# Splitting the output projection of the last three query blocks by head pair in a GroupNorm + attention kernel

## The chip, the cores and the metric

The kernel runs on one core of a Trainium2 chip. The time is device microseconds of one execution; the figure given is the median of the timed runs. A separate profiled execution gives the trace, whose span is a few microseconds shorter than the timed median.

The engines are named as in the profile: PE is TensorE, DVE VectorE, ACT ScalarE, POOL GpSimd, SP SyncE (it issues most transfers). PEld is the loading of weights on TensorE.

## The reference

The input x has the shape (4, 512, 48, 48): four images, 512 channels, T = 2304 positions. Eight heads of 64 channels each.

```python
hn  = group_norm(x, groups=32) * gn_scale + gn_bias
qkv = (einsum('oc,bchw->bohw', qkv_w, hn) + qkv_b)      # fp32
q, k, v = split(qkv.reshape(b, 3, 8, 64, T).astype(float16))
s   = 64 ** -0.25
w   = softmax(einsum('bhct,bhcs->bhts', q * s, k * s))  # T x T per head
a   = einsum('bhts,bhcs->bhct', w, v).astype(float32).reshape(x.shape)
out = einsum('oc,bchw->bohw', proj_w, a) + proj_b
return x + out
```

The change concerns the last two lines: the output projection, its bias and the residual.

## The kernel before

**Tiling.** Two heads form a pair that fills the 128 partitions. There are 4 pairs in each of 4 batches, numbered g = 0 to 15. The queries of a pair are cut into five blocks: j = 0 to 3 with 512 columns and j = 4 with 256. The keys are cut into 18 tiles of 128 rows. A *unit* is three score tiles of one block: matmuls of keys and queries into `ps` (L892), three exponentials of 128x1024 on ACT into `p` (L899), a sum over the key tiles kept on DVE in `acc` (L950, L953), and the matmuls of values into `av` (L917). A block has six units (the last block three), a pair 27, the program 432. A name such as 14_2_5 means pair 14, block 2, unit 5; a slot is the stretch of PE from that unit's scores to the scores of the next.

**The loop.** The list `stream` holds all units in order. Step n issues the scores of unit n, the `acc` addition of unit n-1 and the values of unit n-2 (`BEHIND` = 2). The space beside it is filled by `fill(n)`: it takes *pieces* from the list `beside` in the order in which they were put there, at most one chain that ends per call, at a rate that spreads the remaining work over the units left until it is needed. Every piece has a unit before which it may not start. The pieces are halves of the chains for q and k of a later pair (`qk_chain`, L696), for v (`v_chain`, L741), copies of attention outputs, and projection chains. Between pieces `fill` also runs due transfers and small tasks.

**After the last unit of a block.** `add_up` (L970) sums `acc` over the partitions with matmuls against ones into `sl`; DVE copies it to `slx` (L980); small transfers bring the sums to the layout `sums` (L984); POOL checks their limits (L1008, L1009); DVE inverts them (L1015); a transfer writes `row` to DRAM (L1017), and a second one reads it back, spread over 64 partitions per head, as `ib` (L1027). POOL then multiplies `avx` (the copy of `av`) by `ib` into `att` (L1034). These steps are spread over four later loop steps.

**Projection.** For one block of a batch, `att32` (L813) casts the fp16 `att` of the four pairs to fp32r tiles `a`. Before the change one work tile `a32` with room for all four pairs and with one buffer serves every block except blocks 3 and 4 of the last batch (`at_end`), whose copies lie in freed x tiles. A projection chain is eight matmuls for 128 output channels: four pairs, each with a high and a low half of the weight, `whi` and `wlo` (L819). It goes into one PSUM bank: the single bank of `ps_w` during attention, or a bank of the score tiles when the flag `alone` is set. The evacuation on DVE (L839) adds bias and residual in one pass; the store goes out on SP one step later (L846). The residual is loaded on SP into a tile `r` by `residual`, one chain ahead of its use (L791). The 256-column block packs two output chunks into one bank, so it has two chains of sixteen matmuls.

**The order in the last batch.** The projection of the third batch's blocks runs beside pairs 14 and 15. It is followed by the last batch's own blocks 0, 1 and 2, each released a few steps after the last pair's block is divided. Blocks 3 and 4 come partly or wholly after the last unit: `alone[0] = True`, the last values, `add_up` of the last block, and then the rest of `beside`. In the last pair, blocks 3 and 4 are divided without the way through DRAM (`direct`, L991 to L993): DVE takes the reciprocal of the sums at full width, and POOL or DVE multiplies.

**The end.** The results of the sums check in `fine` are reduced on DVE (L1326), summed over partitions by a matmul (L1328), and compared into `flag` (L1329). A branch on that flag chooses whether the general, slower softmax has to be run; it isn't taken with these inputs.

Of the kernel before, what the change touches and what calls it, by code (L numbers as in the profile page):

```python
# [26 lines left out]
P = 128  # L27
# [440 lines left out]
def fast_path(  # L468
# [113 lines left out]
    fine = const.tile([P, 2, QB // P], F32, name="fine")  # L582
# [197 lines left out]
    def residual(b, j, chunks):  # L780
        n = QBLOCKS[j][1]
        if at_end(b, j):

            tag = f"x{chunks[0]}_{j - NQ + 2}"
            xt = xpool.tile([P, QB], F32, tag=tag, name=f"r_{b}_{j}_{chunks[0]}")
        else:
            xt = work.tile(
                [P, QB], F32, tag="res", bufs=3, name=f"r_{b}_{j}_{chunks[0]}"
            )
        xt = xt.rearrange("p (m n) -> p m n", n=n)  # L790
        nc.sync.dma_start(xt, rows_of(x, b, j, chunks))  # L791
        res[b, j, chunks[0]] = xt

    def at_end(b, j):

        return b == B - 1 and j >= NQ - 2

    def att32(b, j, pairs=range(NC)):
        o, n = QBLOCKS[j]
        if (b, j) not in at32:  # L800
            if at_end(b, j):
                at32[b, j] = [
                    xpool.tile([P, n], F32R, tag=f"x{c}_{j}", name=f"a32_{b}_{j}_{c}")
                    for c in range(NC)
                ]
            else:
                t = work.tile(
                    [P, NC, QB], F32R, tag="a32", bufs=1, name=f"a32_{b}_{j}"
                )
                at32[b, j] = [t[:, c, :n] for c in range(NC)]  # L810
        for c in pairs:
            engine = nc.vector if direct(b * NPAIR + c, j) else nc.gpsimd
            engine.tensor_copy(at32[b, j][c], atts[b * NPAIR + c][:, o : o + n])  # L813

    def proj_chain(b, j, m, ps):
        n = QBLOCKS[j][1]
        for c in range(NC):
            for i, w in enumerate((whi, wlo)):
                nc.tensor.matmul(  # L819
                    ps[:, :n],  # L820
                    w[:, c, bass.ts(m, P)],
                    at32[b, j][c],
                    start=(c == 0 and i == 0),
                    stop=(c == NC - 1 and i == 1),
                )

    def proj_pieces(b, j):


        n = QBLOCKS[j][1]  # L830

        def run(chunks):
            bank = chain_bank(f"pr_{b}_{j}_{chunks[0]}")
            places = [bank[:, i * n : (i + 1) * n] for i in range(len(chunks))]
            for m, ps in zip(chunks, places):
                proj_chain(b, j, m, ps)
            xt = res.pop((b, j, chunks[0]))
            for i, m in enumerate(chunks):
                nc.vector.scalar_tensor_tensor(  # L839
                    xt[:, i], places[i], bproj[:, m : m + 1], xt[:, i], ALU.add, ALU.add  # L840
                )

            loads.append(
                (
                    now[0] + 1,
                    lambda: nc.sync.dma_start(rows_of(out, b, j, chunks), xt),  # L846
                )
            )

        def ahead(k):  # L850
            if k < len(proj_list) and not at_end(b, proj_list[k][0]):
                residual(b, *proj_list[k])

        convert = [
            piece(0.0, lambda: att32(b, j, (NC - 1,) if at_end(b, j) else range(NC)))
        ]
        chains = []
        for k, (jj, chunks) in enumerate(proj_list):
            if jj != j:
                continue  # L860
            chains.append(
                [piece(0.0, lambda k=k: ahead(k)) for k in ([0] if k == 0 else [])]
                + [piece(0.0, lambda k=k: ahead(k + 1))]
                + [piece(QB / 290.0, lambda chunks=chunks: run(chunks), True, True)]
            )
        return convert, chains
# [35 lines left out]
    def values(u):  # L902
        g, j, k, last = u
        b, pr = divmod(g, NPAIR)
        o, n = QBLOCKS[j]
        per = QB // n
        pt = pts.pop(u)
        if k == 0:
            if j == 0:
                atts[g] = apool.tile([P, T], F16, tag="att", name=f"att_{g}")  # L910
            av[0] = ps_av.tile([P, QB], F32, tag="av", name=f"av_{g}_{j}")
        for r in range(BURST):
            for a in range(per):
                i = (k * BURST + r) * per + a
                for h in range(2):
                    lo = h * D
                    nc.tensor.matmul(  # L917
                        av[0][lo : lo + D, :n],
                        vv[b, pr // 2][:, i, pr % 2 * P + lo : pr % 2 * P + lo + D],
                        pt[:, r, h, a * n : (a + 1) * n],  # L920
                        start=(i == 0),
                        stop=(i == NT - 1),
                    )
        if last:
            avx[g, j] = work.tile([P, QB], F32, tag="avx", name=f"avx_{g}_{j}")
            nc.vector.tensor_copy(avx[g, j][:, :n], av[0][:, :n])  # L926

    def direct(g, j):

        return g == NG - 1 and j >= NQ - 2  # L930

    def add(u):
# [6 lines left out]
        if direct(g, j) and (last or j == NQ - 1):  # L939
            acc[g, j].append(pt)  # L940
            return
# [14 lines left out]
    def add_up(g, j):  # L956
# [3 lines left out]
        sl = ps_av.tile([P, QB], F32, tag="av", name=f"sl_{g}_{j}")  # L960
# [6 lines left out]
        for i, (t, r, a) in enumerate(steps):  # L967
            for h in range(2):
# [7 lines left out]
                )  # L976

        def rows():
            sx = work.tile([P, QB], F32, tag="rows", name=f"slx_{g}_{j}")
            nc.vector.tensor_copy(sx[:, :n], sl[:, :n])  # L980

            sm = small.tile([P, 2, QB // P], F32, tag="sums", name=f"sums_{g}_{j}")
            for h in range(2):
                nc.sync.dma_start(sm[:, h, : n // P], sx[h * D : h * D + 1, :n])  # L984
            sums[g, j] = sm
            return sx

        if direct(g, j):
            source = rows() if n == QB else sl
            inv = work.tile([P, QB], F32, tag="rows", name=f"inv_{g}_{j}")  # L990
            nc.vector.reciprocal(inv[:, :n], source[:, :n])  # L991
            engine = nc.vector if source is sl else nc.gpsimd
            engine.tensor_tensor(  # L993
                atts[g][:, o : o + n], avx.pop((g, j))[:, :n], inv[:, :n], ALU.mult
            )
            if source is sl:
                rows()
        else:
            rows()

    def check_sums(g, j):
        n = QBLOCKS[j][1]
        sm = sums[g, j][:, :, : n // P]
        ok = fine[:, :, : n // P]
# [44 lines left out]
    def put_run(run, *args, when=None):  # L1049

        put([piece(0.05, lambda: run(*args), when=when)])
# [61 lines left out]
    def ready(b, j):  # L1113
# [3 lines left out]
        return BEHIND + (2 if j >= NQ - 2 else 5)  # L1117
# [5 lines left out]
    def put_proj(b, j, *which):  # L1123

        end = ends[((b + 1) * NPAIR - 1) * NQ + j]
        for i in which or range(len(projs[b, j][1])):
            put(projs[b, j][1][i], end + ready(b, j) + 1)

    for b in range(B):
# [13 lines left out]
        if b == B - 1:  # L1143
            put_qk(g + 3, 1)
            put_qk(g + 3, 0)
            put_convert(old, 0)
            for j in range(NQ):
# [3 lines left out]
            for j in range(NQ - 2):  # L1151
                put_convert(b, j)
                put_proj(b, j)
                if j < 2:
                    for jj, chunks in proj_list:
                        if jj == NQ - 2 + j:
                            put_run(residual, b, jj, chunks)
                    put_run(att32, b, NQ - 2 + j, range(NC - 1))
            put_convert(b, NQ - 2)
            put_proj(b, NQ - 2)  # L1160
# [82 lines left out]
    def fill(n):  # L1243
# [12 lines left out]
        for us, _, _, _, _, _, need in beside:  # L1256
            work += us
            left = min(need * per_pair, len(stream)) - n
# [23 lines left out]
    end = len(stream)  # L1282
    for n in range(end):
        summed = stream[n - BEHIND - 1][:2] if ended(n - BEHIND - 1) else None
        if summed:
            add_up(*summed)
# [9 lines left out]
        if ended(n - BEHIND - 2):  # L1296
            check_sums(*stream[n - BEHIND - 2][:2])
            if not direct(*stream[n - BEHIND - 2][:2]):
                invert(*stream[n - BEHIND - 2][:2])
        if ended(n - BEHIND - 3) and not direct(*stream[n - BEHIND - 3][:2]):  # L1300
# [8 lines left out]
    alone[0] = True  # L1309
    add(stream[-1])  # L1310
    for u in stream[-BEHIND:]:
        values(u)
    check_sums(NG - 1, NQ - 2)
    add_up(NG - 1, NQ - 1)
    att32(B - 1, NQ - 1, (NC - 1,))
    for pieces in projs[B - 1, NQ - 1][1]:
        beside.extend(pieces)
    while beside:
        issue()
        while loads:  # L1320
            loads.popleft()[1]()
    check_sums(NG - 1, NQ - 1)


    good = small.tile([P, 1], F32, tag="good", bufs=1, name="good")
    nc.vector.tensor_reduce(good, fine.rearrange("p h i -> p (h i)"), AX.X, ALU.add)  # L1326
    pf = chain_bank("count")[:1, :1]
    nc.tensor.matmul(pf, good, ones, start=True, stop=True)  # L1328
    nc.vector.tensor_scalar(flag, pf, float(2 * QB) - 0.5, None, ALU.is_lt)  # L1329
# [57 lines left out]
```

## Time and profile before

| | us |
|---|---|
| median of three timed runs | 1666.96 |
| lowest, highest | 1666.34, 1669.79 |
| span of the profiled execution | 1659.0 |
| PE busy | 1597.6 |
| ACT busy | 1246.5 |
| DVE busy | 1131.3 |
| POOL busy | 370.8 |
| start of the slot of the last unit, 15_4_2 | 1627.93 |
| `flag` written | 1652.22 |

The first rows of the profile give the busy time of each engine. In the groups of instructions each row is a line, an engine, an operation and its operands, with the number, the busy time and the mean of one; what stands at its end is the idle time in front of these instructions and what ended it. The view of waits gives, for an engine, the line that waited, the line that released it, the sum in microseconds, the number of times, and the longest. The chain of waits goes back from the last instruction to what released each step; its rows have start, duration, and what ran. The order of time lists every instruction with the idle time before it in brackets.

### The profile page before, as it was taken

The page shows a single profiled execution, that of the slowest core. Times are in us where ns is not written, and L with a number is a line of the kernel's source. Part 1 is how long each engine was busy: PE and PEld are TensorE (multiplying, and loading weights), DVE is VectorE, ACT ScalarE, POOL GpSimd, SP SyncE. Part 2 cuts the span into 40 slices and gives each one's busy share as a digit, 9 for nine tenths or more (in the row PEclk, how much of TensorE's full clock was granted, in tenths as well). Part 3 has the DMA queues.
Part 4 walks back from the last instruction along what each step waited for, and adds up shares of the span by engine and source line. Part 5 has one row for each costly group of instructions (what it writes and reads, how often), then busy time and mean ns, then how long its engine had stood idle before and what let it go on. Part 6 is the DMA issues. An engine that isn't in the chain of part 4 may idle for free.

```text
span 1659.0 us, 28335 instructions
## 1 busy us (share of the span) xinstructions
PE 1597.6 (96%) x11528; PEld 699.7 (42%) x11528; DVE 1131.3 (68%) x1282; ACT 1246.5 (75%) x1317; POOL 370.8 (22%) x499
## 2 busy tenths in 40 slices
PE   6999999899999999999999999999999999999987
PEld 2533444244333443445433344345533334434445
DVE  4257667887666667878666666887766677676664
ACT  3078788887878877777778777876778888887772
POOL 1002112222121213232111121223111222214241
PEclk9999999999999999999999999999999999999999
DMA  6000002200000002540100000443110000003443
GB/s 215 1 1 23 15 15 65 74 14 17 14 11 14 18 14 60 161 133 17 33 14 11 14 14 11 130 119 112 24 26 11 14 17 15 15 11 124 134 126 120
DMA packets 95184, 82.10 MB, mean 49 GB/s; under 512 B 51140, under 2 KB 61252, under 8 KB 95044
## 3 DMA queue, kind: packets, MB, share of 16 engines
q1 hardware_dynamic: 93572, 79.14, 17.0%
q8 instruction: 92, 1.51, 0.4%
q10 hardware_dynamic: 1344, 1.05, 0.2%
q14 instruction: 48, 0.39, 0.1%
q0 software_dynamic: 128, 0.01, 0.0%
HBM read 60.70 MB, written 19.17 MB: 48 GB/s over the span
## 4 chain that ended last, share of the span: by engine, by line
PE 87%; DVE 4%; DMA 3%; POOL 3%; ACT 2%; issue 1%; SPq 0%; ACTq 0%; DVEq 0%; POOLq 0%
PE pqk L696 28%; PE ps L892 17%; PE av L917 17%; PE pv L741 15%; PE pr L819 7%; POOL a L813 2%; ACT p L899 2%; DVE acc L950 2%; PE ps L696 1%; PE sl L970 1%; DMA row<-inv 1%; DVE acc L953 1%; DMA ib<-row 1%; DMA out_dram<-r 1%; DVE st L605 0%
## 5 line engine op out<-in xcount | busy, mean ns | idle before, releaser
L899 ACT ACTIVATE p<-ps 128x1024 f16<-128x1024 f32 x1296 | 1231.6, 1027 | 360.9 <-PE ps L892 358.4
L950 DVE TENSOR_TENSOR acc<-acc,p 128x3072 f16<-128x3072 f16 x270 | 486.4, 1802 | 69.7 <-ACT p L899 69.0
L696 PE MATMUL pqk<-x,wqkv 128*64 128x512 f32 (+1 forms) x2464 | 518.6, 551 | 0.5 <-DVE k L705 0.4
L892 PE MATMUL ps<-q,k 64*128 64x512 f16 (+1 forms) x2880 | 362.3, 358 | 17.0 <-ACT p L899 14.9
L917 PE MATMUL av<-p,v 128*64 128x512 f16 (+1 forms) x2880 | 361.3, 364 | 0.0
L1008 POOL TENSOR_SCALAR in<-sums 128x8 f32<-128x8 f32 (+1 forms) x160 | 109.7, 686 | 726.3 <-DMA sums<-slx 719.5
L741 PE MATMUL pv<-wqkv,x 128*64 128x256 f32 x2304 | 268.1, 380 | 0.0
L696 PEld LDWEIGHTS pqk<-x,wqkv 128*64 128x64 f32 x2464 | 168.7, 137 | 226.5 <-issue 170.6
L1034 POOL TENSOR_TENSOR att<-avx,ib 128x512 f16<-128x512 f32 (+1 forms) x78 | 132.8, 1703 | 447.0 <-DMA ib<-row 366.1
L892 PEld LDWEIGHTS <-k 64*128 64x128 f16 x2880 | 107.3, 94 | 294.9 <-issue 248.2
L917 PEld LDWEIGHTS <-v 128*64 128x64 f16 x2880 | 131.7, 109 | 209.8 <-issue 165.8
L741 PEld LDWEIGHTS pv<-wqkv,x 128*64 128x64 f32 x2304 | 160.7, 137 | 92.1 <-DVE v L749 5.4
L819 PE MATMUL pr<-a,whi 128*128 128x512 f32 (+1 forms) x320 | 126.5, 403 | 14.0 <-POOL a L813 10.8
L950 DVE TENSOR_TENSOR acc<-p,p 128x3072 f16<-128x3072 f16 x79 | 139.1, 1760 | 0.0
L819 PE MATMUL pr<-a,wlo 128*128 128x512 f32 (+1 forms) x320 | 117.3, 375 | 0.0
L953 DVE TENSOR_TENSOR acc<-acc 128x1024 f16<-128x1024 f16 x156 | 113.3, 726 | 5.3
L705 DVE TENSOR_SCALAR q<-pqk,bqkv 128x512 f16<-128x512 f32 (+1 forms) x79 | 54.9, 695 | 84.2 <-PE pqk L696 83.7
L749 DVE TENSOR_TENSOR v<-pv,bv 128x512 f16<-128x512 f32 x72 | 49.8, 691 | 89.2 <-PE pv L741 88.6
L705 DVE TENSOR_SCALAR k<-pqk,bqkv 128x512 f16<-128x512 f32 (+1 forms) x75 | 52.2, 696 | 80.9 <-PE pqk L696 80.8
L839 DVE SCALAR_TENSOR_TENSOR r<-pr,bproj,r 128x512 f32<-128x512 f32 (+1 forms) x80 | 54.7, 693 | 63.4 <-PE pr L819 56.2
L926 DVE COPY avx<-av 128x512 f32<-128x512 f32 (+1 forms) x80 | 51.0, 637 | 68.6 <-PE av L917 68.4
L819 PEld LDWEIGHTS pr<-a,whi 128*128 128x128 f32 x320 | 60.5, 189 | 56.5 <-POOL a L813 22.6
(61 smaller groups left out, 467.7 us busy)
## 6 DMA issues: line engine op xcount, KB each, us to landing
r<-x_dram SPq DMA_DIRECT2D x72, 256.0 KB, 2.9
out_dram<-r SPq DMA_DIRECT2D x72, 256.0 KB, 3.0
ib<-row SPq DMA_DIRECT2D x126, 128.0 KB, 3.0
x<-x_dram SPq DMA_DIRECT2D x62, 256.0 KB, 4.5
x<-x_dram SPq DMA_DIRECT2D x16, 128.0 KB, 4.7
sums<-slx SPq DMA_DIRECT2D x128, 2.0 KB, 2.1
ib<-row SPq DMA_DIRECT2D x30, 64.0 KB, 2.8
wqkv<-qkv_wT_dram SPq DMA_DIRECT2D x2, 768.0 KB, 6.9
```

The source lines that it names most:

```text
L696: nc.tensor.matmul(pw[0][lo : lo + D, :n], wqkv[:, c, w0 + lo : w0 + lo + D], hn[b, c, j], start=(c == 0), stop=(c == NC - 1),)
L705: nc.vector.tensor_scalar(qk[g][part][:, o : o + n], pw[0][:, :n], bqkv[:, col : col + 1], SCALE, ALU.add, ALU.mult,)
L741: nc.tensor.matmul(pw[0][lo : lo + D, a, :], hn[b, c, i * P // QB][:, at + lo : at + lo + D], wqkv[:, c, 2 * C + half * C // 2 :][:, : C / ...
L819: nc.tensor.matmul(ps[:, :n], w[:, c, bass.ts(m, P)], at32[b, j][c], start=(c == 0 and i == 0), stop=(c == NC - 1 and i == 1),)
L839: nc.vector.scalar_tensor_tensor(xt[:, i], places[i], bproj[:, m : m + 1], xt[:, i], ALU.add, ALU.add)
L892: nc.tensor.matmul(ps[:, h, a * n : (a + 1) * n], kt[rows, bass.ts(i, P)], qt[rows, o : o + n], start=True, stop=True,)
L899: nc.scalar.activation(pt[:, r], ps, AF.Exp)
L917: nc.tensor.matmul(av[0][lo : lo + D, :n], vv[b, pr // 2][:, i, pr % 2 * P + lo : pr % 2 * P + lo + D], pt[:, r, h, a * n : (a + 1) * n], ...
L950: nc.vector.tensor_tensor(t, before, pt, ALU.add)
L953: nc.vector.tensor_tensor(t[:, 0], t[:, 0], t[:, r], ALU.add)
L1008: nc.gpsimd.tensor_scalar(t, sm, limit, None, op)
L1034: nc.gpsimd.tensor_tensor(atts[g][:, o : o + n], avx.pop((g, j))[:, :n], ibs.pop((g, j))[:, :n], ALU.mult,)
```

## The change

The projection of the last batch's blocks 2, 3 and 4 is split into two parts. The first part covers three pairs, which are finished while the last pair still computes its attention: six-matmul chains beside the last pair's attention, whose evacuation adds bias and residual and leaves the sum in SBUF. The second part covers the last pair alone: two matmuls per output chunk, whose evacuation adds PSUM to the stored sum. This is meant to leave less work behind the last attention and to give otherwise empty attention slots something to do.

With it go:

- The fp32r copies are one tile per pair (`a32_0` to `a32_3`), so that a copy has to wait only for the old block's matmuls of the same pair.
- Blocks with copies in x tiles stay blocks 3 and 4 of the last batch (`left_over`), and blocks 2 to 4 keep their residuals in x tiles (`in_two`).
- The first residual of a batch's block 0 is issued together with its copies, a few steps before its chain.
- The rate of `fill` counts units only up to the last but two.
- The tail is rewritten: block 3 of the last pair is divided right after its sums; block 2's second part runs between the last values on the single bank; the last block's sums go into that bank too, and the division reads `av` from PSUM; the last check of sums is made on DVE over all 256 columns; the remaining chains use three double banks of the score tiles; the six stores alternate between SP and ACT; the flag is written after the fourth evacuation.

```diff
-        if (b, j) not in at32:
-            if at_end(b, j):
...
-                t = work.tile(
-                    [P, NC, QB], F32R, tag="a32", bufs=1, name=f"a32_{b}_{j}"
+        for c in pairs:
+            if left_over(b, j):
+                t = xpool.tile([P, n], F32R, tag=f"x{c}_{j}", name=f"a32_{b}_{j}_{c}")
+            else:
+                t = work.tile(
+                    [P, QB], F32R, tag=f"a32_{c}", bufs=1, name=f"a32_{b}_{j}_{c}"
                 )
...
+    FIRST, LAST = range(NC - 1), range(NC - 1, NC)
...
+        def evacuate():
+            if pairs == LAST:
+                ps = bank[:, : len(chunks) * n].rearrange("p (m n) -> p m n", n=n)
+                nc.vector.tensor_tensor(xt, ps, xt, ALU.add)
+            else:
+                for i, m in enumerate(chunks):
+                    bias = bproj[:, m : m + 1]
+                    nc.vector.scalar_tensor_tensor(
+                        xt[:, i], places[i], bias, xt[:, i], ALU.add, ALU.add
+                    )
...
+        def start():
+            att32(b, j, LAST if in_two(b, j) else range(NC))
+            if j == 0:
+                ahead(0)
...
             put_qk(g + 3, 1)
-            put_qk(g + 3, 0)
+            put_qk(g + 3, 0, range(NQ - 1))
             put_convert(old, 0)
+            put_qk(g + 3, 0, (NQ - 1,))
             for j in range(NQ):
                 put_proj(old, j)
                 if j + 1 < NQ:
                     put_convert(old, j + 1)
-            for j in range(NQ - 2):
-                put_convert(b, j)
-                put_proj(b, j)
                 if j < 2:
-                    for jj, chunks in proj_list:
-                        if jj == NQ - 2 + j:
-                            put_run(residual, b, jj, chunks)
-                    put_run(att32, b, NQ - 2 + j, range(NC - 1))
-            put_convert(b, NQ - 2)
-            put_proj(b, NQ - 2)
+                    put_run(residuals, b, NQ - 2 + j)
+                if j >= NQ - 2:
+
+                    there = ends[(NG - 2) * NQ + j] + BEHIND + 6
+                    put_run(att32, b, j, FIRST, after=there)
+            put_first(b, NQ - 2)
+            put_convert(b, 0)
+            put_proj(b, 0)
+            put_run(residuals, b, NQ - 3)
+            put_first(b, NQ - 1)
+            put_convert(b, 1)
+            put_proj(b, 1)
+            put_run(att32, b, NQ - 3, FIRST)
+            put_first(b, NQ - 3)
+            put_convert(b, NQ - 3)
+            put_proj(b, NQ - 3)
             continue
...
-            left = min(need * per_pair, len(stream)) - n
+            left = min(need * per_pair, len(stream) - BEHIND) - n
...
+        if n == late + BEHIND:
+
+            g, j = stream[late][:2]
+            sx = rows(g, j, add_up(g, j))
+            divide_here(g, j, sx, avx[g, j], nc.gpsimd)
...
-    alone[0] = True
     add(stream[-1])
-    for u in stream[-BEHIND:]:
-        values(u)
-    check_sums(NG - 1, NQ - 2)
-    add_up(NG - 1, NQ - 1)
-    att32(B - 1, NQ - 1, (NC - 1,))
-    for pieces in projs[B - 1, NQ - 1][1]:
-        beside.extend(pieces)
-    while beside:
-        issue()
+    values(stream[-2])
+    check_sums(g, NQ - 2)
+    while beside or loads:
         while loads:
             loads.popleft()[1]()
-    check_sums(NG - 1, NQ - 1)
+        if beside:
+            issue()
+    att32(b, NQ - 2, LAST, nc.scalar.copy)
+    values(stream[-1])
+    sl = add_up(g, j, small_bank("sl_last"))
+    divide_here(g, j, sl, av[0], nc.vector)
+    att32(b, j, LAST, nc.vector.tensor_copy)
...
+    ends_of = []
+    for i, (jj, chunks) in enumerate(rest):
+        if i % 2 == 0:
+            banks = ps_s.tile([P, 2, QB], F32, tag="ps", name=f"rest_{i}")
+        ends_of.append(proj_run(b, jj, chunks, LAST, banks[:, i % 2, :]))
+    pf = small_bank("count")[:1, :1]
+    nc.tensor.matmul(pf, good, ones, start=True, stop=True)
+    for i, (evacuate, store) in enumerate(ends_of):
+        evacuate()
+        store(nc.scalar if i % 2 else nc.sync)
+        if i == NC - 1:
+            every = P * fines.shape[1]
+            nc.vector.tensor_scalar(flag, pf, every - 0.5, None, ALU.is_lt)
```

In the changed kernel's order, the copies of the third batch's block 3 stand on POOL behind the divide of pair 14's block 3, and those of the last batch's block 2 (first part) behind the divide of pair 15's block 2; the second-part copy of that block stands behind the multiply of pair 15's block 3.

## The prediction

> **What bounds the kernel now.** I read the page's busy table first, then the chain that ended last, then PE's waits, then the order of time around the places where PE waits.
>
> ```profile
> PE 1597.6 (96%) x11528; PEld 699.7 (42%) x11528; DVE 1131.3 (68%) x1282; ACT 1246.5 (75%) x1317; POOL 370.8 (22%) x499
> PE 87%; DVE 4%; DMA 3%; POOL 3%; ACT 2%; issue 1%; SPq 0%; ACTq 0%; DVEq 0%; POOLq 0%
> ```
>
> TensorE is busy for 96% of 1659.0 us. The matmuls are the same in both kernels (the same rows stream), so the change can win only PE's idle time and the end, after the last attention. Where PE waits:
>
> ```profile
> PE ps L892 <- ACT p L899: 14.9, 33, 0.5
> PE pr L819 <- POOL a L813: 10.8, 13, 1.5
> PE pr L819 <- DVE r L839: 3.3, 3, 2.7
> ```
>
> The first line is attention slots with nothing beside them: scores (0.75) and values (0.77) take 1.52 us, three exps about 2.75, so PE waits 1.2 to 1.3. The second is projections waiting for the fp32r copies of att on POOL. The third is one event:
>
> ```profile
> 677.78 0.84 PE L917 MATMUL av<-p,v 128*64 128x512 f16 x6
> 681.31 0.80 PE L819 MATMUL pr<-a,whi 128*128 128x512 f32 x1 [2.69 <-DVE r L839]
> 681.90 0.63 PE L819 MATMUL pr<-a,wlo 128*128 128x512 f32 x1
> ```
> ```profile
> 674.62 5.75 DMA r<-x_dram
> ```
>
> The chain shows that this evacuation waited for its residual, loaded late. After the idle time the matmuls come every 0.43 us instead of 0.2335, for about 3.4 us: half clock. The end is a serial tail:
>
> ```profile
> 1626.58 1.42 PE sl L970 x12
> 1627.99 0.76 PE ps L892 x12
> 1628.76 2.06 PE pr L819 x8
> 1630.82 2.10 PE av L917 x36
> 1632.92 0.02 issue
> 1632.95 0.44 DVE avx L926
> 1633.38 0.04 issue
> 1633.42 2.16 PE sl L970 x36
> 1635.58 15.24 PE pr L819 x80
> ```
>
> The tail lasts 1659.0 - 1627.93 = 31.07 us, 15.24 of it projection matmuls with no attention to cover.
>
> **What the Trainium skill says.** "TensorE: Matmul & The Clock Gate", Part 1, "What's actually happening": the PE clock halves after an idle window of about 3.4 us; windows run free, so whether a gap triggers it depends on where it falls. The trace agrees for idle times of 2.07 (at 322) and 2.69 (at 681) and shows no drop after 1.51. Its section "Architectural detail" says that ACT, DVE and GpSimd take instructions strictly in order; the trace agrees (casts start only when the divide ahead of them ends, 1597.83 and 1599.04). "GPSIMD Engine Reference", Specifications: POOL shares its SBUF interfaces with VectorE; the trace has the 128x512 cast at 0.56 us beside a quiet DVE and 0.95 to 1.18 beside its accumulations. "DMA: Bandwidth & Descriptors", "Anatomy of one DMA": about 2 us fixed, mostly completion; the trace has 2.6 to 3.3 for row, ib and store.
>
> **The change part by part.**
>
> *Residual (0) of a batch with the copies* (E1). Block 0's first residual is issued in the conversion, slots before its chain, so the load at 674.62 is there in time. The slot at 677.03 took 7.65 us; its normal size with eight projection matmuls is 3.59. It gives 7.65 - 3.59 = 4.06; I take **-3.9**.
>
> *A copy tile per pair* (E2, E3). Today one tile holds four pairs, so a copy waits for the whole previous block's matmuls. With a tile each, copies overlap that block's last chain. Loss in batch 0's blocks near 721: 1.0, of which I take **-0.9**; batch 1's near 1129: 1.7, I take **-1.5**. The losses at 1094 (2.78, POOL behind a divide) and 1112 (1.8, POOL behind a sums check) have another cause and stay.
>
> *Pieces beside the last attention.* In the changed order, one more half qk chain is done before slot 14_2_5 (pair 14, block 2, unit 5), which so starts at 1493.89 + 1.73 = 1495.62. From there to 15_4_1 there are 36 slots: 26 have an eight-matmul chain (2.07), 7 a six-matmul chain (six at 0.2335 and the fill, 1.60), 2 the twelve 256-column matmuls (1.61), one is empty. Work: 36 x 1.52 + 26 x 2.07 + 7 x 1.60 + 3.22 + 3.46 (sums) = 126.4, so 15_4_2 would start at 1622.04 instead of 1627.93: -5.9. Today eight of these slots are empty (10.5 us lost) and POOL copies cost 7.4; the half chain and the 3 x 4 + 3 first-part chains moved here fill them. I add back 1.3 for the empty slot, 0.5 for POOL waits at block 1's last chains, 0.4 for small ACT/DVE waits: **-3.7**.
>
> *New wait X on POOL.* The changed order puts the copies of batch 2's block 3 behind att_14_3, the divide of pair 14's block 3, and the chain of that block's first projection comes two slots after, in 15_0_2. The divide waits for row (DMA), then ib (DMA), and on SP the residual load between them waits for a store to land, as today at 1512.95 (store), 1516.26 (load), 1516.70 (ib). Counted from slot 14_4_2: row 6.85, ib 11.15, divide 14.95 to 16.2 (3.8 from ib's issue to its landing; 1.27 for the divide), four casts of 0.56, chain end about 19.0 us instead of 13.9. Today the same divide is 14.93 after that slot (1544.75), and the copies follow it at 1549.22, with no chain due before. Bounds 4.5 (casts quick) to 6 (divide 1.97, casts 1.0). **+5.1**; PE idles about 4 us, so half clock follows: **+1.2** (0 to 1.7). Queued behind the waiting chain on PE: everything.
>
> *New wait Y.* In the same way, the first-part copies of batch 3's block 2 stand behind att_15_2, whose ib is not blocked by a store. From slot 15_3_3: row 1.9, ib 4.56, divide 8.4 to 10.0, chain end 12.3 instead of 10.3: **+2.0** (1 to 3.5), half clock **+0.35**.
>
> *The tail.* Today 31.07. In the changed one, with t the start of 15_4_2: the sums copy .73, DVE reciprocal 3.35 (row L991) ends at 4.17, POOL multiply 1.27 at 5.5, cast 0.56 at 6.1. Only then can block 2's last-pair chains start (its copy is queued behind that multiply); PE has run dry at t+3.9. Four cycles of two matmuls (0.57), evacuation (0.67 to 0.75) and semaphores on the one bank, 1.55 to 1.6 each: t+12.5. Last values and 36 sum matmuls (2.16): t+14.6. Then reciprocal 1.76, multiply 0.43, cast 0.28, checks 1.3, six evacuations at about 0.7, issue 0.5: +8.6. The rest matmuls (8 x 0.2335 + 8 x 0.1175 = 2.8) lie beside the checks. After the last store the page has 6.87 today and the same is expected. Sum 30.1, with some semaphores 30.3: **-0.8**. Half the load on PE in t+3.9 to t+12.5 is idle, so a half-clock spell is likely here: **+1.7** (0 to 4).
>
> *Costed at nothing:* residual loads of the later blocks (SP idle, DMA busy share 0.3 to 0.5); the last first-part evacuations (DVE busy 20 of 31 us, hidden behind PE); the sums check off POOL; stores on ACT's queue (ACT idle after the last exp).
>
> Sum: -3.9 - 0.9 - 1.5 - 3.7 + 6.3 + 2.35 - 0.8 + 1.7 = **-0.45**. On 1666.96 this is 1666.5.
>
> **The rivals.**
>
> A (forecast): filled slots and earlier loads win about 10.8, the order on POOL and the clock give back about 10.3. 1666.5.
>
> B, faster: X and Y are hidden. For it: ib may be issued before the residual load, or the store land earlier (row to ib takes 2.5 to 2.7 us where nothing blocks it, 4.2 to 4.4 where it does); without the block X shrinks by 1.7 and its clock spell goes with 1.2, Y and tail spells are absent (0.35 + 1.7). Against it: today's divide already lands at 14.93. Then 1666.5 - 5 = 1661.5.
>
> C, slower: the half clock lasts in the tail (+4 instead of 1.7), X is 6 and Y 3.5, or a first-part chain waits for its predecessor's evacuation. For it: single-bank chains with idle gaps in which PE is busy for less than half the time. Against: attention slots before it run PE near full. 1666.5 + 2.3 + 0.9 + 1.5 = 1671.2.
>
> **How the numbers follow.** A 0.43, B 0.37, C 0.20. A lies within 0.2% (3.3 us), B beyond it on one side, C on the other. The range reaches from just under B to C: 1660.5 to 1671.3.
>
> **What would show it.** Right: no wait for r near 677; a long PE wait for POOL a some 13 us after slot 14_4_2, with PEclk under 1 behind it; another in slot 15_3_5; few waits of ps for p after 1497; 15_4_2 near 1624.5 in the changed trace; from there to the end about 30 to 32 us, with PE idle for 2 us before block 2's last-pair chains. Wrong: X under 2 us would mean B; a tail over 33 us would mean C; E1 fails if the first residual's landing is still late.

## The result, and the profile after

The changed kernel takes 1678.47 us (median of four runs, 1676.88 to 1680.37) against 1666.65 for the kernel before (four runs here; the 1666.96 further up is the median of the first three): 11.8 us more, a ratio of 1.0069 with a 95% interval of 1.0050 to 1.0088. It is slower by 0.7%, and outside the predicted range of 1660.5 to 1671.3.

The first rows of the page of the changed kernel, busy time by engine and the shares of the chain that ended last:

```profile
PE 1607.4 (96%) x11528; PEld 704.5 (42%) x11528; DVE 1139.7 (68%) x1292; ACT 1248.1 (74%) x1318; POOL 354.8 (21%) x495
PE 85%; DVE 6%; DMA 4%; issue 2%; POOL 1%; ACT 1%; SPq 0%; ACTq 0%; DVEq 0%; POOLq 0%
```

The number of matmuls is the same, 11528, but they are busy for 9.8 us longer (1597.6 before), since a matmul at half clock takes longer. The two traces lie further apart than the medians, 1659.0 against 1678.6 us of span: the traced execution before was 6 us under its median, the one after 1.9 over. The other 9.8 of these 19.6 us are idle time of PE. PE's waits, in the same view as before (who waited, for whom; sum, times, longest):

```profile
PE pr L820 <- POOL a L812: 17.0, 8, 7.7
PE ps L913 <- ACT p L920: 7.2, 16, 0.5
PE pr L820 <- DVE r L847: 6.9, 8, 1.6
PE pr L820 <- DVE r L843: 2.4, 3, 0.8
```

The wait for exps went from 14.9 to 7.2, because the change filled attention slots as intended. The wait for copies rose from 10.8 to 17.0, one of 7.7 among them, and the wait for evacuations from 3.3 to 9.3 (6.9 and 2.4).

The durations of the stages show where the time went. They are worked out from the starts of slots in the order of time on PE, as in the prediction; "last pairs" is from 14_2_5 to 15_4_2, "tail" from 15_4_2 to the end. The kernel before was profiled a second time (run `before_2` below), since its first traced execution, 1660.7 us, lies 6 us under the median; the second took 1666.8.

| stage, us | before | before, second | after | predicted (a sign means a change) |
|---|---|---|---|---|
| batch 0's projection (22 slots from 677) | 88.7 | 89.8 | 87.9 | -4.8 |
| batch 1's projection (30 slots) | 115.0 | 115.5 | 113.4 | -1.5 |
| from there to 14_2_5 | 325.1 | 325.1 | 326.9 | +1.7 |
| last pairs | 134.0 | 137.8 | 150.5 | 137.3 |
| tail | 31.1 | 30.9 | 32.5 | 32.0 |
| span | 1659.0 | 1665.0 | 1678.6 | |

The 137.3 is the sum on record: 126.4 of work, 2.2 of small waits, X with its clock 6.3, Y 2.35. Against the second trace of before the last pairs are 12.7 us longer, the tail 1.7, and the rest comes to -0.8. So the cause lies in the last pairs. Their 36 slots took 24.1 us more than the 126.4 of work; 10.9 of that were on record. A slot's loss is its duration less the matmuls that ran in it at full clock:

| loss in the last pairs, us | on record | measured |
|---|---|---|
| X: slot 15_0_2, with its clock | 6.3 | 9.4 |
| Y: slot 15_3_5 and the next, with their clock | 2.35 | 4.45 |
| the third batch's block 4, two slots, with their clock | nothing | 4.1 |
| a chain that waits for the evacuation ahead of it, five slots | 0.4 (small waits for ACT and DVE) | 4.5 |
| the empty slot | 1.3 | 1.6 |
| copies at block 1's last chains | 0.5 | 0.0 |

The largest piece is the slot 15_0_2. On PE, in order of time:

```profile
1551.13 0.79 PE L820 MATMUL pr<-a,whi 128*128 128x512 f32 x1 [7.74 <-POOL a L812]
1551.72 0.63 PE L820 MATMUL pr<-a,wlo 128*128 128x512 f32 x1
1552.15 0.63 PE L820 MATMUL pr<-a,whi 128*128 128x512 f32 x1
```

After 7.74 us of idle time the chain comes every 0.43 us, half clock, for all of its eight matmuls: the slot takes 13.01 instead of 3.59. On POOL (the wait X, copies behind the divide) and on SP's queue (start, duration, line, transfer) in the same kernel:

```profile
1549.26 1.26 POOL L1050 TENSOR_TENSOR att<-avx,ib 128x512 f16<-128x512 f32 x1 [8.85 <-DMA ib<-row]
1550.47 2.29 POOL L812 CAST a<-att 128x512 fp32r<-128x512 f16 x4
```
```profile
1540.32 0.38 SPq L1033 DMA_DIRECT2D row<-inv  x1
1540.75 0.46 SPq L852 DMA_DIRECT2D out_dram<-r  x1
1544.83 0.33 SPq L791 DMA_DIRECT2D r<-x_dram  x1
1545.27 1.12 SPq L1043 DMA_DIRECT2D ib<-row  x2
```

The copies do wait for a divide that waits for `ib`. But `ib` was issued only at 1545.27, since SP stood for about 4 us in front of a residual load whose buffer was just being stored; and `row` itself went out at 1540.32, which is 10.9 us after slot 14_4_2 (1529.39) and not 6.85 as worked out. (In the kernel before it is 8.5, 1538.34 after 1529.82, so that 6.85 was low even for that kernel.) The chain of waits tells what made `row` late:

```profile
1526.91 3.19 DMA out_dram<-r
1530.10 0.02 issue
1530.12 5.25 DMA r<-x_dram
...
1535.49 0.06 DVE r L847
...
1539.32 0.15 DVE inv L1031
```

A residual load waited for a store (3.19) and took 5.25 to land among three other loads; the evacuation on DVE waited for it, and behind that evacuation stand additions to `acc` and then the reciprocal `inv`. A second way ends at the same moment. The sums that `inv` needs were ready on DVE at 1530.90, but SP issued their transfer only at 1536.42 (1530.97 in the kernel before): it stood for 5.1 us in front of one more residual load, until a store had landed.

```profile
1530.55 0.38 SPq L852 DMA_DIRECT2D out_dram<-r  x1
1536.04 0.33 SPq L791 DMA_DIRECT2D r<-x_dram  x1
1536.42 1.14 SPq L1005 DMA_DIRECT2D sums<-slx  x2
```
```profile
1539.29 0.24 POOL L1024 TENSOR_SCALAR in<-sums 128x8 f32<-128x8 f32 x1 [11.49 <-DMA sums<-slx]
```

Both ways lead through SP's queue. The view of SP's own waits between 1495 and 1580 us, where the third batch is projected, shows that this is no single event; the kernel before, then the changed one:

```profile
SPq L791 <- DMA out_dram<-r: 16.7, 8, 2.8
```
```profile
SPq L791 <- DMA out_dram<-r: 38.6, 14, 5.1
```

### The profile page after: what moved, and what is told of

Same layout as the page of the kernel before. It is cut to its first block, busy times and chain, and to the rows that moved or that the text cites. A ratio compares the mean times of both kernels' runs of the same rounds, so it can differ in the third digit from the quotient of the medians.

```text
span 1678.6 us, 28355 instructions
## 1 busy us (share of the span) xinstructions
PE 1607.4 (96%) x11528; PEld 704.5 (42%) x11528; DVE 1139.7 (68%) x1292; ACT 1248.1 (74%) x1318; POOL 354.8 (21%) x495
## 3 DMA queue, kind: packets, MB, share of 16 engines
q8 instruction: 92, 1.51, 0.4%
q10 hardware_dynamic: 1904, 1.84, 0.4%
## 4 chain that ended last, share of the span: by engine, by line
PE 85%; DVE 6%; DMA 4%; issue 2%; POOL 1%; ACT 1%; SPq 0%; ACTq 0%; DVEq 0%; POOLq 0%
PE pqk L696 28%; PE ps L913 17%; PE av L938 17%; PE pv L741 15%; PE pr L820 6%; DMA out_dram<-r 2%; DVE acc L967 2%; PE ps L696 1%; PE sl L989 1%; DVE acc L970 1%; DMA ib<-row 1%; ACT p L920 1%; POOL a L812 1%; DVE st L605 1%; DMA r<-x_dram 0%
## 5 line engine op out<-in xcount | busy, mean ns | idle before, releaser
L1024 POOL TENSOR_SCALAR in<-sums 128x8 f32<-128x8 f32 (+1 forms) x158 | 103.8, 657 | 733.1 <-DMA sums<-slx 726.6
L1050 POOL TENSOR_TENSOR att<-avx,ib 128x512 f16<-128x512 f32 (+1 forms) x78 | 127.3, 1632 | 482.3 <-DMA ib<-row 437.8
L970 DVE TENSOR_TENSOR acc<-acc 128x1024 f16<-128x1024 f16 x156 | 119.3, 765 | 5.3
L705 DVE TENSOR_SCALAR q<-pqk,bqkv 128x512 f16<-128x512 f32 (+1 forms) x79 | 55.0, 696 | 87.9 <-PE pqk L696 87.4
```

The source lines that it names most:

```text
L705: nc.vector.tensor_scalar(qk[g][part][:, o : o + n], pw[0][:, :n], bqkv[:, col : col + 1], SCALE, ALU.add, ALU.mult,)
L970: nc.vector.tensor_tensor(t[:, 0], t[:, 0], t[:, r], ALU.add)
L1024: nc.gpsimd.tensor_scalar(t, sm, limit, None, op)
L1050: nc.gpsimd.tensor_tensor(atts[g][:, o : o + n], avx.pop((g, j))[:, :n], ibs.pop((g, j))[:, :n], ALU.mult,)
```

## The experiments

Two theories were set against each other. S: the in-order queue on SP, where a residual load waits for the store of the same buffer in front of it, sets the pace, and `row`, `ib`, divide and copies come late behind it. P: it is the order on POOL, copies behind a divide. Every ratio is against the kernel before on the same chip, whose median is in the third column. Differences to the changed kernel are those of the medians. The changed kernel was not run again beside them, and its own interval is 6 us wide, so each of these differences is uncertain by about 3 us; counted from the kernel before on the same chip, they would be 6.2 for `a_swap` (7.5 below), 7.0 for `a_order` (8.3 below), and within 0.5 of what is given for the others. Stages come from one trace of each run, which lies up to 3.6 us off the run's median.

| run | median, us | before | ratio to before (95%) | last pairs | tail |
|---|---|---|---|---|---|
| changed kernel | 1678.47 | 1666.65 | 1.0069 (1.0050 to 1.0088) | 150.5 | 32.5 |
| a_swap | 1670.96 | 1665.33 | 1.0031 (1.0019 to 1.0044) | 145.2 | 32.1 |
| a_order | 1670.17 | 1665.33 | 1.0026 (1.0019 to 1.0034) | 142.0 | 32.6 |
| a_x5 | 1669.99 | 1666.59 | 1.0024 (1.0014 to 1.0035) | 139.6 | 32.3 |
| a_5buf | 1670.20 | 1667.01 | 1.0025 (1.0016 to 1.0034) | 139.2 | 32.4 |
| a_late | 1676.35 | 1667.01 | 1.0045 (1.0029 to 1.0061) | 145.8 | 32.4 |
| a_tail | 1668.09 | 1666.59 | 1.0012 (1.0006 to 1.0019) | 148.5 | 23.6 |
| a_all | 1649.35 | 1666.59 | 0.9896 (0.9872 to 0.9919) | 130.2 | 23.7 |
| b_swap | 1668.35 | 1665.33 | 1.0018 (1.0005 to 1.0031) | 136.1 | 37.3 |
| b_e1 | 1663.02 | 1665.33 | 0.9988 (0.9979 to 0.9997) | 136.0 | 31.3 |
| b_pair | 1660.99 | 1666.59 | 0.9968 (0.9960 to 0.9976) | 135.2 | 30.8 |
| b_cured | 1660.83 | 1667.01 | 0.9959 (0.9944 to 0.9973) | 133.8 | 30.6 |
| before_2 | 1666.76 | 1667.01 | one run | 137.8 | 30.9 |

**Load ahead of store.** The residual's piece moves to the step of its own chain, and stores go out at the end of a step:

```diff
-                [piece(0.0, lambda k=k: ahead(k + 1)), proj_piece(b, j, chunks, pairs)]
+                [piece(0.0, lambda k=k: ahead(k + 1), True), proj_piece(b, j, chunks, pairs)]
...
-                loads.append((now[0] + 1, store))
+                stores.append((now[0] + 1, store))
...
             closed = closed or last
+        send(n)
```

> The changed kernel with one order changed on SP: the residual load of the next chain is issued ahead of the store of the last one, so that it no longer waits in the queue for a store that was issued just before it out of the same buffer. Theory S (the in-order SP queue sets the pace of the projection chains; what waits behind it, row and ib, comes late and so do the sums, the divide and the copies): PE's waits for DVE r fall from 6.9 us in 8 to under 1.5, the wait for POOL a in slot 15_0_2 from 7.7 to about 3.5, the time falls by 9 to 14 us, to 1665 to 1669. Theory P (the order on POOL alone, copies behind a divide): the wait in 15_0_2 stays over 6 us, the time falls by less than 4.

The time fell by 7.5 us, less than S said and more than P, and the wait in 15_0_2 fell to 5.3 only. Waits for DVE r stayed, 6.6 us in 11, and SP still waited for stores between 1495 and 1580 us, 26.9 us in 12. An instance on SP's queue of this run:

```profile
1504.48 2.43 SPq L792 DMA_DIRECT2D r<-x_dram  x5
1506.95 0.43 SPq L853 DMA_DIRECT2D out_dram<-r  x1
1507.65 0.38 SPq L1034 DMA_DIRECT2D row<-inv  x1
1512.51 0.33 SPq L792 DMA_DIRECT2D r<-x_dram  x1
```

Behind five loads issued at once the store at 1506.95 took 5.5 us to land, and the next load for that buffer waited for it all the same. The swap leaves one slot of slack, and here that was not enough. So the run is inconclusive between the two.

> The kernel before with the same order on SP (load ahead of store). Theory S: its waits for DVE r (3.3 us in 3) go, with the half clock at 681, and the divides come earlier: 3 to 7 us faster than before. Theory P: within 1.5 us of before, since its waits for POOL a come from the shared copy tile.

No gain, 3.0 us slower. The comparison is spoilt by the tail: 37.3 instead of 31.1 us, since the swap makes a late residual of the last block: PE waits 3.5 us for a copy that stands on DVE behind the evacuation which needs that residual. The projection stages of batches 0 and 1 and the last pairs lie within 1 to 2 us of the two traces of before, on either side. SP's waits for stores between 1495 and 1580 us did not fall but rose, from 16.7 to 23.9 us. Nothing here speaks for S in the kernel before, where slots without chains leave the queue room; the run can't exclude it either.

**Five buffers.** Two x tiles that are free in the last batch serve as further residual buffers for the third batch (`a_5buf`); `a_late` moves the split blocks' residual loads; `a_x5` does both.

```diff
+        elif b == B - 2 and proj_list.index((j, chunks)) % 5 > 2:
+            tag = f"x{proj_list.index((j, chunks)) % 5 * 2 - 5}_1"
+            xt = xpool.tile([P, QB], F32, tag=tag, name=f"r_{b}_{j}_{chunks[0]}")
```
```diff
-                if j < 2:
-                    put_run(residuals, b, NQ - 2 + j)
+                for m in {NQ - 2: (0, 1), NQ - 1: (2, 3)}.get(j, ()):
+                    put_run(residual, b, NQ - 2, (m,))
...
             put_first(b, NQ - 2)
+            put_run(residuals, b, NQ - 1)
```

> The changed kernel with five instead of three buffers for the residuals of the third batch's projection (two freed x tiles added), and the split blocks' residual loads one or two at a time after the stretch of the third batch's chains instead of four at once within it. SP order otherwise as in the changed kernel. Theory S (stores and residual loads set the pace): between 1495 and 1575 PE's waits for DVE r go, and the wait for POOL a in slot 15_0_2 falls from 7.7 to under 4.5; 6 to 11 us faster than the changed kernel. Theory P (POOL's order): 7.7 stays above 6; less than 4 us faster.

> The changed kernel with the two extra residual buffers for the third batch alone; the split blocks' residual loads stay where the change put them, four at once in the middle of that stretch. If the reuse of a buffer (a load that waits in SP's queue for the store in front of it) is what costs, all of the 8.5 us that both edits brought together: 7 to 9 us faster than the changed kernel. If the four loads at once are it, 0 to 3 us.

> The changed kernel with the split blocks' residual loads moved behind the third batch's chains and three buffers as in the change. If the four loads at once crowd out the stores, 5 to 9 us faster than the changed kernel and the wait for POOL a in 15_0_2 falls to about 5; if buffer reuse alone is it, 0 to 3 us.

`a_5buf` is 8.3 us faster than the changed kernel, `a_x5` 8.5, `a_late` 2.1, which is within the uncertainty. With five buffers SP never waits for a store between 1495 and 1580 us, in `a_5buf` or in `a_x5`; in `a_late` it still does, 40.3 us in 15. So it is the reuse of the buffer that costs, and not the four loads at once. SP's queue in `a_5buf`, the same stretch:

```profile
1538.16 0.38 SPq L1036 DMA_DIRECT2D row<-inv  x1
1538.58 0.47 SPq L855 DMA_DIRECT2D out_dram<-r  x1
1539.09 0.44 SPq L794 DMA_DIRECT2D r<-x_dram  x1
1541.13 1.12 SPq L1046 DMA_DIRECT2D ib<-row  x2
```
```profile
1546.66 0.50 PE L823 MATMUL pr<-a,whi 128*128 128x512 f32 x1 [3.51 <-POOL a L815]
```

The load follows its neighbour store after 0.5 us instead of 4.1, `ib` follows `row` after 3.0 instead of 5.0, and the wait X is 3.51: about the 4 us that the prediction gave it (3.8 in `a_x5`). So about half of the idle time in X came from SP's queue. In `a_late` it was still 7.48.

**POOL's order.** The rule that divides the last pair's blocks one step earlier is taken out:

```diff
-            if n >= end - per_pair:
-                divide(*stream[n - BEHIND - 3][:2])
```

> The changed kernel with every divide on POOL issued one step later, as for the earlier pairs, so that the copies of the third batch's block 3 and the first-part copies of the last batch's block 2 stand ahead of the divides. Theory P: both long waits for POOL a (7.7 and 2.7) go with the half clock after them, 10 to 13 us faster than the changed kernel. Theory S: the wait moves: the chain starts, but its evacuation has no residual until the blocked load lands, so PE waits for DVE r instead; 4 to 8 us faster.

8.3 us faster, at the upper end of what S said. The waits of 7.7 and 2.7 are gone, although SP waits for stores as long as before (39.0 us in 14): the idle time in X needs both, the divide ahead of the copies and the slow queue ahead of the divide. Waits for DVE r rose from 6.9 to 10.7 us, as S said, and a new wait for copies appeared:

```profile
1562.97 1.96 POOL L1050 TENSOR_TENSOR att<-avx,ib 128x256 f16<-128x256 f32 x1 [8.19 <-DMA ib<-row]
1564.88 5.06 POOL L812 CAST a<-att 128x256 fp32r<-128x256 f16 x10
```

The later divide of pair 14's block 4 now stands right ahead of the copies of the third batch's block 4, and PE waited 4.53 us there, with half clock after it.

**The tail.**

```diff
-            put_first(b, NQ - 3)
+            put_first(b, NQ - 3, (0, 1))
             put_convert(b, NQ - 3)
+            put_first(b, NQ - 3, (2, 3))
...
+    alone[0] = True
     while beside or loads:
```

> The changed kernel with two edits in the tail: the second-part copy of the last batch's block 2 is issued two chains earlier, so that it stands ahead of the multiply of pair 15's block 3, and block 2's second-part chains use the double banks of the score tiles instead of the single bank. Prediction's tail step: 2.1 us of waiting for that copy, about 1.0 of each of four cycles and the half clock after them (sum matmuls 3.95 instead of 2.16) go, so 5 to 8 us faster than the changed kernel; if the DVE reciprocal of 3.35 and the evacuations behind it set the tail instead, 0 to 3 us.

10.4 us faster, the tail 23.6 us instead of 32.5, more than expected. The chain of waits of the changed kernel and of `a_tail` over the same work, each from block 2's last-pair chains to the sums:

```profile
1652.26 0.75 PE pr L820 x2
1653.01 0.02 issue
1653.03 0.70 DVE r L843
1653.73 0.04 issue
1653.78 1.24 PE pr L820 x2
...
1659.02 1.42 PE av L938 x12
1660.44 3.76 PE sl_last L989 x36
```
```profile
1645.15 2.18 PE pr L820 x8
1647.33 0.78 PE av L938 x12
1648.11 1.98 PE sl_last L989 x36
```

On one bank, matmuls and evacuation take turns. The first cycle, at full clock, takes 1.5 us and the next two 2.0, at half clock, which lasts through the 36 sum matmuls: 3.76 instead of 1.98. On several banks the eight matmuls run through in 2.18. From the start of 15_4_2 to the end of the sums it is 18.1 us in the changed kernel and 9.0 in `a_tail`. Of the 9.1 between them, the wait for the copy is 2.1, the turns 4.6 (with their clock), and the clock of the last values and the sums 2.4. The run made both edits at once, so it does not show which of the two brought the half clock. The Trainium skill, "TensorE: Matmul & The Clock Gate", section "A second HAM failure mode: psum-queue depth-cycling", tells of a kernel where short idle times between groups of matmuls come often enough for the clock to go back and forth. Here idle times of 0.78 us stand between the groups at half clock, but one of 2.12 us comes ahead of them, and no run has the short ones alone.

**All of it**, with each divide issued behind its step's chain, so that the copies of the third batch's blocks 3 and 4 stand ahead of the divides of pair 14's:

> The changed kernel with five residual buffers, the split loads, the tail's two edits, and every divide issued one step later and behind that step's chain. If theories S and P and the tail each carry a part, this is 16 to 22 us faster than the changed kernel, 1656 to 1663 and so faster than before; if the clock is what costs, it stays within 5 us of before.

1649.35 us: 29.1 us faster than the changed kernel and 17.2 faster than before, more than expected. The three separate gains (8.5, 8.3 and 10.4) add to 27.2, the same within the uncertainty, though the order here goes a step further than in `a_order`. PE's waits for copies on POOL, 17.0 us in the changed kernel, are 0.8 in the whole run. The windows of the last pairs and the tail (length, then busy time of PE, PEld, DVE, ACT and POOL with counts, granted clock, DMA share, GB/s), the changed kernel and then `a_all`:

```profile
1495.55:1646.06 150.51, 132.96 (x798) 70.92 (x798) 93.67 (x99) 102.78 (x109) 46.19 (x65) 0.95 0.38 119
1646.06:1678.60 32.54, 17.06 (x118) 11.27 (x116) 14.75 (x21) 3.47 (x4) 2.70 (x6) 0.72 0.24 84
```
```profile
1494.10:1624.30 130.20, 127.07 (x798) 68.77 (x796) 93.86 (x99) 102.79 (x109) 48.44 (x66) 1.00 0.47 137
1624.30:1648.00 23.70, 12.40 (x118) 9.23 (x116) 14.43 (x21) 3.48 (x4) 2.19 (x5) 0.81 0.33 116
```

The same 798 matmul records take 130.2 instead of 150.5 us, at a clock of 1.00 instead of 0.95: 3.8 over the 126.4 of work that the prediction counted.

**Parts alone in the kernel before.** `b_e1` issues the first residual with the copies, `b_pair` has a copy tile per pair, `b_cured` has both and the five buffers.

> The kernel before with only the first residual of a batch issued together with the copies. The prediction's step E1 says 3.9 us faster. Theory S: the slot at 677 shrinks by 4 us, but the next chains then run into the store-then-load pace and wait for DVE r within the next 40 us; 0 to 1.5 us faster.

2.3 us faster: over S's figure, under the step's 3.9. In its one trace batch 0's projection takes 89.0 us, between the 88.7 and 89.8 of before, so the stage itself doesn't show the gain. The wait of 2.69 is gone, and a wait of 1.55 for DVE r came in the slot at 704, where the kernel before has none. In the changed kernel too (694 to 726 us) four such waits sum to 2.8. The chain of waits of the changed kernel shows what holds one of them, and it isn't the store:

```profile
690.63 3.56 DMA sums<-slx
...
694.28 0.14 DVE inv L1031
...
695.37 0.66 DVE r L847
```

The evacuation stands on DVE behind other work, a reciprocal among it that waits for the sums to land.

> The kernel before with one copy tile per pair in place of one for all four. The prediction's steps E2 and E3 say 2.4 us faster, more beside the last attention, where POOL copies cost 5.3: up to 5 us faster. Theory S: copies come earlier, but the chains then run at the pace of stores and loads; 0 to 2 us faster.

5.6 us faster, a little above what the prediction's steps allow and well above S. PE's waits for copies fell from 10.8 to 6.4 us. Where the time was won isn't shown: the traced execution was 3.6 us over the run's median, and its last pairs, 135.2, lie between those of the two traces of before.

> The kernel before, projection not split and tail as it was, with three small parts: a copy tile per pair, the first residual issued with the copies, five residual buffers for the third batch. If the split itself is worth what it was made for, this stays 7 us or more above the changed kernel with all cures (1649.4): 1656 to 1661. If the cures are all, it comes within 3 us of 1649.

6.2 us faster. `a_all` is 11.5 us under `b_cured`, 3.5 in the last pairs and 6.9 in the tail by the traces. So the change with its cures is worth more than the cures without it. The 11.5 are the split, the rewritten tail and the order of the divides together; no run has the split alone.

> The kernel before, unchanged, profiled once more, to see how far one trace of it lies from another: the stretch from 14_2_5 to 15_4_2 took 134.0 and the tail 31.1 in the first; both within 2 us in the second, and differences elsewhere only in spells of lower clock.

The tail is within 0.3 us, the last pairs 3.8 apart, more than expected: two waits for copies (1.42 at 1502 and 1.70 at 1608) were each followed by a spell of half clock that the first trace did not have.

## Why the prediction was wrong, step by step

The step that failed is the line "costed at nothing: residual loads of the later blocks (SP idle ...)". With it fell the "row 6.85" of X, and a wait of the same kind as X was not named. The parts, with what they measured:

- **E1, E2, E3 (-3.9, -0.9, -1.5).** In batch 0 the stage changed by -0.8 against the first trace and -1.9 against the second, where -4.8 was said. The wait at 677 went, as E1 said, but alone it gave 2.3 us: the next evacuations come late on DVE and take part of it back. In batch 1 the -1.5 came (115.0 to 113.4), in part by luck. The loss of 1.7 at 1129 is gone, as E3 said, and so it is in `b_pair`; but the 1.8 at 1112, which were to stay, are gone too, and the loss near 1094 grew from 2.8 to 4.4 (4.2 in the second trace of before).
- **Pieces beside the last attention (-3.7).** The slots were filled as counted (26, 7 and 2 chains, one slot empty), and a chain of eight that waited for nothing ran at 3.59 us a slot. (The "3 x 4 + 3" chains of that passage don't fit its own sum, which has 7 + 2 first-part chains; the sum is right.) What failed is the cost of nothing for the residual loads. With a chain in almost every slot, a load that waits for the store of its own buffer holds SP's queue, for 2.8 us on average and up to 5.1, in slots of 3.6 us. The prediction counted this once, for `ib` in X, and not for the whole stretch. Chains that waited for evacuations lost 4.5 us here. Five buffers, which end all those waits on SP, took 8.3 us of the run back.
- **X (+5.1 and +1.2).** Right in kind and place. The slot lost 9.4 us instead of 6.3. The term that failed is "row 6.85": it was 10.9, since SP's queue held both the residual ahead of `inv` on DVE and the sums that `inv` inverts. With the queue free the idle time was 3.5 instead of 7.7.
- **A wait not named.** The third batch's block 4 has the same order, copies behind the divide of pair 14's block 4: 1.84 us of waits and a slowed clock, 4.1 us in two slots.
- **Y (+2.0 and +0.35).** Idle time 2.66, the slot 3.07 over; the next slot lost 1.4 more to the clock. Size low by 2.
- **The tail (-0.8 and +1.7).** 32.5 against 32.0, partly by luck. The start of block 2's last-pair chains was right: t+6.1 was said, and 1652.26 is t+6.2. From there the sum has t+14.6 for the end of the sums, 16.3 with the clock; it was t+18.1, since the second and third cycles took 2.0 instead of 1.55 to 1.6 and the last values, 1.4 us, had no term of their own. What follows up to the last evacuation took 7.5 instead of 8.6.
- **The signs.** The waits in 15_0_2 and 15_3_5, the slots without waits for exps and the 2 us of idle time before block 2's chains came. 15_4_2 "near 1624.5" came at 1646.06; the prediction's own terms give 1626.6 for it (1627.93 - 6.3 - 3.7 + 6.3 + 2.35).
- **Rival C** had the right side, X went past its figure and Y came near it, but its sign, a tail over 33, did not come (32.5), and its sum, 4.2 over before, did not hold the queue's pace either.
- **The clock.** The prediction set a window of about 3.4 us beside idle times of 2.07 and 2.69 and read this as agreement. It isn't agreement: both are shorter than that window, and half clock followed both, as it did 1.42 and 1.70 in the second trace of before.

What is not settled: the split between idle time and clock. Whether half clock follows a given wait changed from run to run, and no run here held the clock apart from the waits. Nor is it shown how the 8.3 us of the five buffers divide between X and the evacuations.

## What to carry to other kernels

When a change fills the empty slots of a steady stretch, look at the queues that lived on those slots: a load that reuses the buffer of the store just ahead of it holds everything behind it in the queue until the store has landed. Count what is issued per slot on every in-order queue, SP included, before a transfer is costed at nothing. On an engine that works in order, put the instruction that waits for a transfer behind those whose inputs are there already. And give chains of short matmuls several banks: on a single one they took turns with the evacuations, 4.6 us for four chains here.

## What the runs showed of the hardware

- The idle time that brings half clock has no fixed size here. Waits of 2.66 and 7.74 us were both followed by 3.4 to 3.7 us of it; in the second trace of before, waits of 1.42 and 1.70 were followed by it as well, each with a shorter wait close by. In the first trace 1.51 was not, and in the changed kernel 1.50 and 1.55 were not. In the tail, 2.12 us and then three gaps of 0.78 were followed by half clock from 1653.8 to 1664, about 10 us.
- Between 1495 and 1580 us a 256 KB store took 2.3 us to land in the kernel before and 3.1 in the changed one (medians), and a load 2.9 and 3.1. Single ones took longer: 5.5 for the store behind five loads of the same size in `a_swap`, 5.25 for a load beside three others.
